# Selective scans in two layers: two groups prepared together, with the bands at other steps

## The chip, the cores and the metric

The kernel runs on one core of a Trainium2 chip. The metric is the device time of one execution in microseconds, and of several executions the median is given. The kernel has four layers; the change touches the selective scans of the first two, which the code calls layer 0 and layer 1.

## The reference, cut to what matters

Both layers contain a two-dimensional selective scan. An image of 56 x 56 tokens is read in four directions: by rows, by columns, and both backwards. For each direction kd, channel d and state n (16 states) the reference does, over the 3136 tokens in turn:

```
dts, Bs, Cs = split(x_proj @ xs)             # per direction
delta = softplus(dt_proj @ dts + bias)
dA    = exp(delta * A[d, n])
h     = dA * h + (delta * x) * B[n]          # the recurrence
y     = sum over n of h * C[n]               # then + D * x
```

Layer 0 does this for two images of 256 channels, one image after the other. Layer 1 has four heads, one after the other; in each, two images of 64 channels lie side by side on the 128 partitions. The layers after these (attention, spectral filters, a mixture of experts) aren't touched.

## The kernel before, in words

The class `Scans` serves both layers. `nch` is the number of blocks of 128 channels: 2 in layer 0, 1 in layer 1. The 3136 tokens of a direction are cut into four quarters of 784 tokens; a direction and a quarter make a *group*, so that one run has 16 groups, in the order of directions 0, 2, 1, 3. Directions 0 and 2 go along rows, 1 and 3 along columns; the latter add their sums to y through a transposed view. A group takes 16 *steps* for each channel block, one step for each state n: 32 steps in layer 0, 16 in layer 1. There are two runs in layer 0 and four in layer 1, 2048 steps in all.

One step, over a tile of 128 x 784, is spread over the engines like this:

- ScalarE makes the decay a = exp(A delta) into one of two PSUM buffers (`decay`, L318).
- TensorE spreads row n of B over the partitions into the PSUM tile b (`spread`, L343). There is one such buffer. VectorE multiplies it by du (L396). For the five states in `POOLED` (2, 5, 8, 11, 14) a DMA brings B's row instead and GpSimd multiplies (L412).
- VectorE runs the recurrence (`scan`, L337).
- ScalarE keeps the last column of h for the next quarter (L329).
- GpSimd multiplies h by C's row, which two DMAs (one in layer 0) have brought, giving p (L409).
- TensorE adds p into the PSUM tile acc by a product with the identity (`add_up`, L357). At a *job boundary*, every 16 steps, ScalarE takes the sum out (L377) and TensorE begins the next one (L371).

The order of instructions on each engine is written out by hand: `emit(s)` issues for step s the decay of step s+1, the scan of s, the spread of s+2, the rows of C for s+3 and of B for s+6, and so on. Each engine takes its own part of that list in order. SP issues the DMAs.

While a group runs, the next one is *prepared*: `pieces_of` gives the pieces, and `preparation` gives each a step, counted from the start of the running group. A piece has place 0 (in the middle of `emit`, with the PSUM tile b as its buffer) or place 2 (at the end of `emit`). The pieces are:

- `rows`: the projection of x to the rows of dt, B and C, taken to SBUF as xd (L161 on TensorE, L173 on ScalarE).
- `keep`: xd goes to DRAM (L177), from which the rows of B and C are read later.
- `fetch`: the rows of B and C come back in another shape, as the tile whole (L184).
- `band` and `rest`: whole is split into three bfloat16 bands that sum to it. `band` casts on ScalarE (L187), `rest` subtracts on GpSimd (L190), and the next band needs that difference.
- `store` and `spread`: the bands go to DRAM (L194) and come back as the tile three (L200), from which TensorE spreads B.
- `steps`: the product for delta (L161), taken out with its bias on ScalarE (L206).
- `soft`: softplus of delta on ScalarE (L209). Softplus and exp are in different tables of ScalarE, so a load stands ahead of it and another ahead of the next exp. In layer 0 the two channel blocks stand together.
- `copy` and `times`: x through the identity into b (L161), and du = delta x on VectorE (L218).

In layer 1 a group has 16 steps, and each group has a preparation of its own with its own softplus.

The pool `rot` gives the tiles delta and du, nch + 1 buffers of each. xd, whole and the bands have one buffer, three has two. The DRAM pool has three buffers for each name.

Of the kernel before, what the change touches and what calls it, by code (L numbers as in the profile page):

```python
# [14 lines left out]
F32 = mybir.dt.float32  # L15
# [15 lines left out]
NS = 16  # L31
# [3 lines left out]
class Chip:  # L35


    def __init__(self, ctx, tc):
        self.tc, self.nc = tc, tc.nc
        nc = tc.nc  # L40
        const = ctx.enter_context(tc.tile_pool(name="const", bufs=1))
        self.ident = const.tile([128, 128], F32, name="ident")
        make_identity(nc, self.ident)
        self.eps = const.tile([128, 1], F32, name="eps")
        nc.gpsimd.memset(self.eps, 1e-5)
        self.one = const.tile([128, 1], F32, name="one")
        nc.gpsimd.memset(self.one, 1.0)
        self.ones = const.tile([1, 128], F32, name="ones")
        nc.gpsimd.memset(self.ones, 1.0)
        self.X = const.tile([TP, NT, B, C], F32, name="X")  # L50
        self._turn = 0
# [54 lines left out]
class Scans:  # L106
# [13 lines left out]
    def __init__(self, k, ctx, nch, row, col, y, w, side=None):  # L120
        tc = k.tc
        self.k, self.nch, self.row, self.col, self.y, self.w = k, nch, row, col, y, w
        self.rot = ctx.enter_context(k.pool("scan0", nch + 1, side=side))
        self.bands = ctx.enter_context(k.pool("scan2", side=side))
        self.threes = ctx.enter_context(k.pool("scan1", 2, side=side))
        self.dram0 = ctx.enter_context(
            tc.tile_pool(name="scan0d", bufs=1, side=side, space=bass.MemoryType.DRAM)
        )
# [8 lines left out]
    def open(self, ctx):  # L137
        k, nch = self.k, self.nch
        self.once = ctx.enter_context(k.pool("scan4", 1))
        self.two = ctx.enter_context(k.pool("scan5", 2))  # L140
        self.hp = ctx.enter_context(k.pool("scanh", 6))
        self.pp = ctx.enter_context(k.pool("scanp", 4))
        self.cp = ctx.enter_context(k.pool("scanc", 4))
        self.bp = ctx.enter_context(k.pool("scanb", 2))
        self.dram = ctx.enter_context(k.tc.tile_pool(name="scand", bufs=3, space=bass.MemoryType.DRAM))
        self.pa = [ctx.enter_context(k.pool(f"pdec{i}", psum=True)) for i in range(2)]
        self.pb = ctx.enter_context(k.pool("prow", psum=True))
        self.pc = ctx.enter_context(k.pool("psum", psum=True))
# [100 lines left out]
        for ci in range(self.nch):  # L249
            f["times"](ci, False)  # L250

    def preparation(self, g):


        f = self.pieces_of(g, lambda name, n: self.once.tile([128, n], F32, name=name), self.dram)
        if self.nch == 1:
            at = [
                (0, 0, "rows", [0, 1]), (3, 0, "steps", 0, [0, 1]), (9, 2, "soft", 0), (12, 0, "copy", 0),
                (12, 2, "times", 0),
            ]  # L260
            s = 1
        else:
            at = [
                (0, 0, "rows", [0]), (3, 0, "rows", [1]), (12, 0, "steps", 0, [0, 1]), (16, 0, "steps", 1, [0, 1]),
                (20, 2, "soft", 0), (20, 2, "soft", 1), (22, 0, "copy", 0), (22, 2, "times", 0), (25, 0, "copy", 1),
                (25, 2, "times", 1),
            ]
            s = 5
        at += [
            (s, 2, "keep"), (s + 2, 2, "fetch"), (s + 4, 2, "band", 0), (s + 4, 2, "rest", 0),  # L270
            (s + 5, 2, "band", 1), (s + 5, 2, "rest", 1), (s + 6, 2, "band", 2), (s + 7, 2, "store"),
            (s + 10, 2, "spread"),
        ]
        return [(t[0], t[1], f[t[2]], t[3:]) for t in sorted(at, key=lambda t: t[0])]

    def on_all(self, pool, g, name, r):

# [11 lines left out]

    def all_steps(self):  # L290
        steps, self.pieces = [], {}
        for i, g in enumerate(self.groups):
            todo = self.preparation(self.groups[i + 1]) if i + 1 < len(self.groups) else []
            for t in todo:
                self.pieces.setdefault((len(steps) + t[0], t[1]), []).append(t)
            for ci in range(self.nch):
                job = dict(g=g, ci=ci)
                steps += [dict(job=job, g=g, ci=ci, n=n, s=len(steps) + n) for n in range(NS)]
        self.state = {}
        self.steps = steps  # L300
        for s in range(-6, len(steps) + 4):
            self.emit(s)
# [1668 lines left out]
```

## Time and profile before

| what | value |
|---|---|
| median of three runs | 9334.89 us (9326.28 to 9335.70) |
| profiled execution | 9324.35 us, span 9322.6 us |
| TensorE busy | 8134.1 us, 87% |
| VectorE busy | 7120.7 us, 76% |
| ScalarE busy | 3895.4 us, 42% |
| GpSimd busy | 6332.5 us, 68% |
| scans of layer 0 | two runs, in about 110 to 1440 and 1500 to 2800 us |
| scans of layer 1 | four runs, between about 2940 and 5910 us |
| softplus (L209) | 128 of 853 ns, 96 table loads of 1283 ns |
| bands (L187) | 270 of 355 ns; idle before: 272.6 us for the subtraction on GpSimd, 223.3 us for the fetch |
| fetch (L184) | 90, median 5.0 us from issue to landing |

The shares of busy time are means over the whole span. The scans take its first two thirds; in these VectorE and GpSimd are busy, later TensorE is. A row of a group gives the number of instructions, the busy time, the mean length of one, and the idle time of the engine just before them with what ended it. "us to landing" runs from the issue of a DMA to its arrival.

### The profile page before, as it was taken

The page shows a single profiled execution, that of the slowest core. Times are in us where ns is not written, and L with a number is a line of the kernel's source. Part 1 is how long each engine was busy: PE and PEld are TensorE (multiplying, and loading weights), DVE is VectorE, ACT ScalarE, POOL GpSimd, SP SyncE. Part 2 cuts the span into 40 slices and gives each one's busy share as a digit, 9 for nine tenths or more (in the row PEclk, how much of TensorE's full clock was granted, in tenths as well). Part 3 has the DMA queues.
Part 4 walks back from the last instruction along what each step waited for, and adds up shares of the span by engine and source line. Part 5 has one row for each costly group of instructions (what it writes and reads, how often), then busy time and mean ns, then how long its engine had stood idle before and what let it go on. Part 6 is the DMA issues. An engine that isn't in the chain of part 4 may idle for free.

```text
span 9322.6 us, 94373 instructions
## 1 busy us (share of the span) xinstructions
PE 8134.1 (87%) x28825; PEld 4783.3 (51%) x28825; DVE 7120.7 (76%) x7587; ACT 3895.4 (42%) x6609; POOL 6332.5 (68%) x4023
## 2 busy tenths in 40 slices
PE   7888888888888888888888888699999999999998
PEld 3444445444444434444443444345588888874555
DVE  8999998999996997998899799711366676765442
ACT  4555545555545555554555555333211111114331
POOL 5999996999994996998799699666411111115551
PEclk9999999999998999999999899699999999999998
DMA  5666664666663884886688488200233333320003
GB/s 156 221 221 215 215 205 132 221 220 215 213 214 93 224 214 127 221 219 168 173 222 214 124 222 215 77 6 4 61 97 104 101 102 95 109 61 7 14 5 127
DMA packets 781383, 1364.60 MB, mean 146 GB/s; under 512 B 133213, under 2 KB 406494, under 8 KB 780842
## 3 DMA queue, kind: packets, MB, share of 16 engines
q1 hardware_dynamic: 780874, 1358.56, 50.8%
q8 instruction: 229, 3.75, 0.2%
q14 instruction: 280, 2.29, 0.1%
HBM read 1318.63 MB, written 39.60 MB: 146 GB/s over the span
## 4 chain that ended last, share of the span: by engine, by line
PE 49%; DVE 21%; issue 12%; ACT 9%; POOL 4%; DMA 4%; SPq 1%; DVEq 0%; POOLq 0%; ACTq 0%
PE cv L1499 12%; DVE h L337 10%; PE acc L357 7%; DVE h L396 7%; PE av L1011 5%; PE sc L1017 5%; PE pj L1613 4%; ACT a L318 3%; PE b L161 3%; DMA c<-rows 2%; PE acc L371 2%; POOL p L409 2%; PE pcv L438 1%; PE b L343 1%; DMA whole<-rows 1%
## 5 line engine op out<-in xcount | busy, mean ns | idle before, releaser
L409 POOL TENSOR_TENSOR p<-h,c 128x784 f32<-128x784 f32 x2048 | 3763.0, 1861 | 232.9 <-PE acc L357 157.4
L357 PE MATMUL acc<-p,ident 128*128 128x392 f32 x8192 | 3133.6, 513 | 88.8 <-POOL p L409 85.1
L337 DVE TENSOR_TENSOR_SCAN h<-a,state,h 128x784 f32<-128x784 f32 x1536 | 2798.0, 1841 | 86.1 <-ACT a L318 64.9
L357 PEld LDWEIGHTS acc<-p,ident 128*128 128x128 f32 x8192 | 1518.0, 197 | 1179.9 <-POOL p L409 200.9
L396 DVE TENSOR_TENSOR h<-du,b 128x784 f32<-128x784 f32 x1408 | 1335.8, 949 | 177.0 <-PE b L343 173.1
L318 ACT ACTIVATE a<-delta,L0A 128x784 f32<-128x784 f32 x1024 | 938.8, 919 | 837.7 <-DVE h L337 835.8
L412 POOL TENSOR_TENSOR h<-du,b 128x784 f32<-128x784 f32 x640 | 1188.9, 1858 | 3.4 <-DMA b<-rows 3.4
L343 PE MATMUL b<-three,sel 96*128 96x512 bf16 (+1 forms) x2816 | 709.3, 333 | 547.7 <-DVE h L396 503.1
L318 ACT ACTIVATE a<-delta,L1A 128x784 f32<-128x784 f32 x1024 | 936.5, 917 | 534.0 <-DVE h L337 531.8
L1030 POOL TENSOR_TENSOR total<-total,e 128x448 f32<-128x448 f32 (+1 forms) x644 | 734.8, 1141 | 328.3 <-ACT e L1019 289.0
L337 DVE TENSOR_TENSOR_SCAN h<-a,h 128x784 f32<-128x784 f32 x512 | 902.0, 1780 | 44.1 <-ACT a L318 27.5
L1512 DVE TENSOR_TENSOR u<-u,cv 128x512 f32<-128x512 f32 x1024 | 623.8, 682 | 326.9 <-PE cv L1499 325.6
L343 PEld LDWEIGHTS <-sel 96*128 96x128 bf16 x2816 | 276.3, 98 | 1159.9 <-issue 919.7
L1543 POOL TENSOR_TENSOR u<-u,S 128x1024 f32<-128x1024 f32 x64 | 150.1, 2367 | 1043.6 <-DVE S L1512 1043.6
L1019 ACT ACTIVATE e<-sc 128x448 f32<-128x448 f32 (+1 forms) x700 | 376.9, 542 | 727.9 <-PE sc L1017 596.0
L1514 ACT COPY u<-cv 128x512 f32<-128x512 f32 x256 | 149.3, 586 | 827.0 <-PE cv L1499 773.4
L1613 PE MATMUL pj<-u,Wm 128*128 128x196 f32 (+8 forms) x1536 | 354.3, 384 | 5.7 <-DVE A L1619 5.7
L1017 PE MATMUL sc<-big 128*128 128x448 f32 (+1 forms) x700 | 324.0, 549 | 12.3 <-ACT e L1019 12.3
L1011 PE MATMUL av<-e,big 128*128 128x448 f32 (+1 forms) x700 | 322.4, 547 | 1.1 <-DVE e L1024 1.0
L187 ACT CAST bands<-whole 128x196 bf16<-128x196 f32 x270 | 95.8, 355 | 531.3 <-POOL whole L190 272.6
L1593 POOL TENSOR_TENSOR both<-mpm 128x512 f32<-128x512 f32 x32 | 40.6, 1268 | 390.3 <-DVE Wm L1649 271.7
L1613 PEld LDWEIGHTS pj<-u,Wm 128*128 128x128 f32 x1536 | 268.4, 192 | 71.4 <-issue 46.0
(438 smaller groups left out, 10998.0 us busy)
## 6 DMA issues: line engine op xcount, KB each, us to landing
c<-rows SPq DMA_DIRECT2D x1024, 392.0 KB, 4.0
c<-rows SPq DMA_DIRECT2D x2048, 196.0 KB, 4.4
b<-rows SPq DMA_DIRECT2D x320, 392.0 KB, 4.5
b<-rows SPq DMA_DIRECT2D x640, 196.0 KB, 4.5
H<-raw SPq DMA_DIRECT2D x32, 1568.0 KB, 7.4
wC<-win SPq DMA_DIRECT2D x64, 576.0 KB, 6.3
w<-in_L_weight_dram SPq DMA_DIRECT2D x52, 512.0 KB, 5.3
wA<-win SPq DMA_DIRECT2D x64, 384.0 KB, 5.3
```

Of the source, the lines that this page charges most:

```text
L318: self.k.nc.scalar.activation(x["a"], g["delta"][ci], AF.Exp, scale=self.w["A"](g["kd"], ci, x["n"]))
L337: self.k.nc.vector.tensor_tensor_scan(h, a, h, start, ALU.mult, ALU.add)
L343: self.k.nc.tensor.matmul(ps[:, c0:c1], lhsT=self.w["selB"](x["n"]), rhs=x["g"]["three"][:, c0:c1], start=True, stop=True)
L357: nc.tensor.matmul(job["acc"][:, i, 0:392], lhsT=self.k.ident, rhs=x["p"][:, 392 * i : 392 * (i + 1)], start=False, stop=n == NS - 1,)
L396: nc.vector.tensor_tensor(one["h"], one["g"]["du"][one["ci"]], one["b"], ALU.mult)
L409: nc.gpsimd.tensor_tensor(now["p"], now["h"], now["c"], ALU.mult)
L412: nc.gpsimd.tensor_tensor(three["h"], three["g"]["du"][three["ci"]], three["b"], ALU.mult)
L1011: nc.tensor.matmul(acc, lhsT=V[b][:n, j, :], rhs=e[:n], start=j == 0, stop=j == NKT - 1)
L1017: nc.tensor.matmul(ps[:n], lhsT=keys[b][:, KT * j : KT * j + n], rhs=q, start=True, stop=True)
L1030: nc.gpsimd.tensor_tensor(total[:n], total[:n], e[:n], ALU.add)
L1499: self.k.nc.tensor.matmul(ps[:, b], lhsT=v[:, C * b : C * (b + 1)], rhs=h, start=i == 0, stop=i == len(terms) - 1)
L1613: nc.tensor.matmul(ps[:, lo - c0 : hi - c0], lhsT=Ws[f][:, eo, r, :], rhs=u[:, b, f, lo - a0 : hi - a0], start=f == 0, stop=f == 1,)
```

## The change

In layer 1 the groups after the first are prepared two at a time, during the 32 steps of the two groups before; the first group, with 16 steps, hosts the preparation of the next two. Both softplus pieces of a pair stand at one step, so that one visit to the softplus table serves two groups. The last group is a set of its own. In both layers the bands come later after their fetch and stand two steps apart (in layer 1's first set, the first of the two keeps them one step apart). The buffers grow to match: three of delta and du in layer 1 too, four in DRAM.

```diff
-        self.rot = ctx.enter_context(k.pool("scan0", nch + 1, side=side))
+        self.rot = ctx.enter_context(k.pool("scan0", 3, side=side))
...
-        self.dram = ctx.enter_context(k.tc.tile_pool(name="scand", bufs=3, space=bass.MemoryType.DRAM))
+        self.dram = ctx.enter_context(k.tc.tile_pool(name="scand", bufs=4, space=bass.MemoryType.DRAM))
...
-    def preparation(self, g):
-        f = self.pieces_of(g, lambda name, n: self.once.tile([128, n], F32, name=name), self.dram)
-        if self.nch == 1:
-            at = [
-                (0, 0, "rows", [0, 1]), (3, 0, "steps", 0, [0, 1]), (9, 2, "soft", 0), (12, 0, "copy", 0),
-                (12, 2, "times", 0),
-            ]
-            s = 1
-        else:
-            at = [
-                (0, 0, "rows", [0]), (3, 0, "rows", [1]), (12, 0, "steps", 0, [0, 1]), (16, 0, "steps", 1, [0, 1]),
-                (20, 2, "soft", 0), (20, 2, "soft", 1), (22, 0, "copy", 0), (22, 2, "times", 0), (25, 0, "copy", 1),
-                (25, 2, "times", 1),
-            ]
-            s = 5
-        at += [
-            (s, 2, "keep"), (s + 2, 2, "fetch"), (s + 4, 2, "band", 0), (s + 4, 2, "rest", 0),
-            (s + 5, 2, "band", 1), (s + 5, 2, "rest", 1), (s + 6, 2, "band", 2), (s + 7, 2, "store"),
-            (s + 10, 2, "spread"),
-        ]
-        return [(t[0], t[1], f[t[2]], t[3:]) for t in sorted(at, key=lambda t: t[0])]
+    def preparation(self, groups, short):
+        def bands(keep, fetch, band, apart, store, spread):
+            yield from ((keep, 2, "keep"), (fetch, 2, "fetch"), (store, 2, "store"), (spread, 2, "spread"))
+            for i in range(3):
+                yield band + apart * i, 2, "band", i
+                if i < 2:
+                    yield band + apart * i, 2, "rest", i
+
+        def du(at, ci):
+            return [(at, 0, "copy", ci), (at, 2, "times", ci)]
+
+        if self.nch == 2:
+            lists = [[
+                (0, 0, "rows", [0]), (3, 0, "rows", [1]), *bands(5, 8, 11, 2, 16, 19), (12, 0, "steps", 0, [0, 1]),
+                (16, 0, "steps", 1, [0, 1]), (20, 2, "soft", 0), (20, 2, "soft", 1), *du(22, 0), *du(25, 1),
+            ]]
+        elif short:
+            lists = [
+                [(0, 0, "rows", [0, 1]), *bands(1, 3, 5, 1, 8, 11), (3, 0, "steps", 0, [0, 1]), (10, 2, "soft", 0), *du(12, 0)],
+                [(6, 0, "rows", [0, 1]), *bands(7, 9, 12, 2, 17, 20), (9, 0, "steps", 0, [0, 1]), (10, 2, "soft", 0), *du(16, 0)],
+            ]
+        else:
+            lists = [
+                [(0, 0, "rows", [0, 1]), *bands(1, 4, 7, 2, 12, 15), (3, 0, "steps", 0, [0, 1]), (20, 2, "soft", 0), *du(22, 0)],
+                [(6, 0, "rows", [0, 1]), *bands(7, 13, 17, 2, 22, 31), (16, 0, "steps", 0, [0, 1]), (20, 2, "soft", 0), *du(25, 0)],
+            ]
+        at = []
+        for g, todo in zip(groups, lists):
+            f = self.pieces_of(g, lambda name, n: self.once.tile([128, n], F32, name=name), self.dram)
+            at += [(t[0], t[1], f[t[2]], t[3:]) for t in todo]
+        return sorted(at, key=lambda t: t[0])
...
-        for i, g in enumerate(self.groups):
-            todo = self.preparation(self.groups[i + 1]) if i + 1 < len(self.groups) else []
-            for t in todo:
+        more = 2 // self.nch
+        sets = [self.groups[:1]] + [self.groups[i : i + more] for i in range(1, len(self.groups), more)]
+        for i, groups in enumerate(sets):
+            for t in self.preparation(sets[i + 1], i == 0) if i + 1 < len(sets) else []:
                 self.pieces.setdefault((len(steps) + t[0], t[1]), []).append(t)
-            for ci in range(self.nch):
-                job = dict(g=g, ci=ci)
-                steps += [dict(job=job, g=g, ci=ci, n=n, s=len(steps) + n) for n in range(NS)]
+            for g in groups:
+                for ci in range(self.nch):
+                    job = dict(g=g, ci=ci)
+                    steps += [dict(job=job, g=g, ci=ci, n=n, s=len(steps) + n) for n in range(NS)]
```

In the text A and B are the first and the second group of a pair, and steps of a pair's preparation are counted from the start of the 32 steps that host it.

## The prediction

> **What bounds the kernel now.** I read the groups first, then the busy time by stretch, then VectorE's waits in the same stretches, then single groups in the timeline.
>
> The two costliest rows that every scan step passes through (columns: line, engine, operation, tiles, count, busy us, mean ns, idle before and its releaser):
>
> ```profile
> L409 POOL TENSOR_TENSOR p<-h,c 128x784 f32<-128x784 f32 x2048 | 3763.0, 1861 | 232.9 <-PE acc L357 157.4
> ...
> L337 DVE TENSOR_TENSOR_SCAN h<-a,state,h 128x784 f32<-128x784 f32 x1536 | 2798.0, 1841 | 86.1 <-ACT a L318 64.9
> ```
>
> GpSimd and VectorE are matched. The timeline gives the real spacings: a VectorE step with product and scan repeats every 2.62 us, a step with a scan alone (5 of 16) every 1.74 us; GpSimd's products follow one another at 1.81 us. I cut the trace at du (L218), which falls once per preparation, so that each stretch holds whole groups (columns: us; PE, weight loads, VectorE, ScalarE, GpSimd busy; clock; DMA share; GB/s).
>
> ```profile
> 1579.00:2131.00 552.00, 456.54 (x1429) 230.07 (x1428) 538.79 (x394) 284.08 (x500) 541.40 (x309) 0.99 0.69 221
> ...
> 3756.00:4039.00 283.00, 234.57 (x716) 119.82 (x715) 270.30 (x197) 155.59 (x266) 273.92 (x162) 0.94 0.86 225
> ```
>
> The first is layer 0, directions 0 and 2: 7 groups of 32 steps, 78.9 us for 32 steps, prepared with one softplus visit. The second is layer 1, same directions: 7 groups of 16 steps, 80.9 us for 32. The transposed directions 1 and 3 (2294 to 2703, 4080 to 4335) take 81.8 and 85.0 per 32. Both engines are busy over 95%, so what can be won is the few per cent of stalls. VectorE's waits in the four stretches, in the order layer 0 direct, layer 0 transposed, layer 1 direct, layer 1 transposed (total us, times, longest):
>
> ```profile
> DVE h L337 <- ACT a L318: 14.2, 22, 1.1
> ```
> ```profile
> DVE h L396 <- PE b L343: 21.8, 10, 3.0
> ```
> ```profile
> DVE h L337 <- ACT a L318: 9.8, 9, 2.5
> DVE h L337 <- ACT state L329: 1.7, 4, 0.7
> ```
> ```profile
> DVE h L396 <- PE b L343: 15.4, 6, 3.5
> DVE h L337 <- ACT state L329: 3.6, 6, 0.7
> DVE h L337 <- ACT a L318: 3.0, 6, 0.9
> ```
>
> Per 32 steps that is 2.0, 4.7, 3.5 and 7.3 us (with the small rows left out here: 1.9 in the second, 0.9 in the third). Taken off 78.9, 81.8, 80.9, 85.0 this leaves 76.9, 77.1, 77.4, 77.7: one base. So VectorE's work plus its stalls is the time, and layer 1 has 1.5 (direct) and 2.6 us (transposed) more stall per 32 steps than layer 0.
>
> **Where the stalls sit.** Bands, layer 1 (columns: start, us, engine, line, ..., idle before):
>
> ```profile
> 3780.77 0.35 ACT L187 CAST bands<-whole 128x196 bf16<-128x196 f32 x1 [4.47 <-DMA whole<-rows]
> ...
> 3781.97 1.85 DVE L337 TENSOR_TENSOR_SCAN h<-a,state,h 128x784 f32<-128x784 f32 x1 [1.50 <-ACT a L318]
> ```
>
> The first band stands two steps behind its fetch, which was issued at 3775.24 and landed 5.5 us later. ScalarE waits at the band, the next exp is queued behind it, the scan starts 1.50 late. Such a stall appears in every direct group (0.5 to 2.5 us), about 1.3 each, 2.6 per pair. The next bands wait 0.76 and 1.03 us for the subtraction on GpSimd.
>
> The job boundary, transposed:
>
> ```profile
> 3420.71 3.13 PE L371 MATMUL acc<-big,ident 128*128 128x392 f32 x4 [1.37 <-ACT big L377]
> ...
> 3425.26 0.91 ACT L206 ACTIVATE delta<-b,L1dtb 128x784 f32<-128x784 f32 x1 [3.05 <-PE b L161]
> ...
> 3426.92 0.97 DVE L396 TENSOR_TENSOR h<-du,b 128x784 f32<-128x784 f32 x1 [1.92 <-PE b L343]
> ```
>
> The take-out of the last sum, the slow first matmuls of the next, the "steps" product right behind them at step 3, its delta on ScalarE, and only then the single PSUM buffer b is free for the spread that VectorE needs. One such stall per layer-1 group, 15.4/6 = 2.6 us.
>
> The double softplus visit exists already, in layer 0:
>
> ```profile
> 1652.00 1.60 ACT L209 ACTIVATE delta<-delta 128x784 f32<-128x784 f32 x2
> ...
> 1655.87 1.85 DVE L337 TENSOR_TENSOR_SCAN h<-a,state,h 128x784 f32<-128x784 f32 x1 [1.00 <-ACT a L318]
> ```
>
> It takes 1650.71 to 1654.92, 4.2 us with its two table loads, and costs the scan 1.0 in direct groups, nothing in transposed ones, where VectorE has just lost 1.47 at the boundary. A single visit in layer 1 takes 3.4 us and costs 0.3 to 0.7.
>
> **What the skill says.** "ScalarE: Activation LUTs", What ACT_TABLE_LOAD costs: a load takes about 1283 ns plus a drain of about 1380. The trace has 1283 and, between the neighbours, no such drain: exp, load, softplus, load, exp stand with gaps of 0.02 us. I use 1.28. "DMA: Bandwidth & Descriptors", Rules for kernel authors: what reads an earlier DMA's write must wait for its completion, and a fixed cost is hidden by issuing early and waiting late. That is the chain keep, fetch, band; here the fetch's median landing is 5.0 us, well over the 2 us that Anatomy of one DMA fits for its fixed cost.
>
> **The change, part by part**
>
> 1. *Half the visits.* Per layer-1 run 15 visits in the scan loop become 8: 28 fewer in all, 56 table loads, 28 x 2 x 1.28 = 72 us of ScalarE. ScalarE is idle 45% of the stage, so only the stall counts: 1.0 for a double visit against 2 x 0.3 to 0.7. I take nothing.
> 2. *First band later.* Three or four steps behind the fetch instead of two. A wait of 4.5 us falls to about 2 (A) or below nothing (B), and 2 us is what ScalarE has to spare (where nothing else stands between, an exp waits 1.6 us for its scan, and the 4.47 above cost the scan 1.50, so some 3 are free). Gain up to 2.6 per direct pair. The bands two steps apart remove the waits of 1 us on GpSimd.
> 3. *Boundaries.* Of two boundaries in 32 steps only A's keeps "steps" at step 3; B's product is at 16, before the boundary at 18, as in layer 0, where that boundary costs 1.47. Transposed: 2.6 x 2 = 5.2 becomes 2.6 + 1.5 = 4.1. The state and exp rows, 6.6/3 = 2.2 per pair, fall to about 0.5. Gain 2.8 per pair.
> 4. *Crowding.* ScalarE has delta at 16, B's bands at 17, 19, 21 and the visit at 20. Bands are 0.35 us each. The band at 21 stands between exp 22 and exp 23; exp 23 ends 1.45 us after exp 22 and its scan is due 1.84 after, so it is covered; without that cover 0.35 per pair. I keep 0.5 in reserve per pair.
> 5. *DMAs and buffers.* Keeps, fetches, stores and spreads are as many as before. On SP, keep to fetch grows from two steps to three or six, so the queue of c and b rows behind stands less; store follows the last band by one step as before. Spread B at 31 serves step 46. Third delta and du buffers and a fourth DRAM buffer are needed because two groups are prepared while two run; they add no instruction. Nothing.
> 6. *The first group* of each run now hosts two preparations in 16 steps: one more du (0.9), two subtractions (1.0), about 1 of stall: +3 us. The pair before the last group hosts one instead of two: -4.
> 7. *Layer 0.* Its bands move from 9, 10, 11 to 11, 13, 15. Band stalls there are 7.2 us over 7 direct groups, 1.0 each; transposed 0.4.
>
> Sum. GpSimd limits the direct gain: 42 products at 1.81 and 4 subtractions at 0.51 are 78.0 per pair, so I put direct pairs at 79.0, 1.9 less. Transposed pairs: 2.6 less. Per layer-1 run: three direct pairs 5.7, a mixed one 2.2, two transposed 5.2, the last 4, first group -3: 14 us, times four 56. Layer 0: 0.6 x 8 + 0.3 x 7 = 7 per run, two runs 14. In all 70 us: the profiled execution, 9324.35 (span 9322.6), goes to 9254. It lies 10.5 below the median of the three runs, 9334.89; taken off the median, 9265. I say 9263.
>
> **Rivals**
>
> - *GpSimd is the bound in direct groups.* It idles 9 us in seven groups, 2.6 per pair, mostly under "PE acc". If those gaps stay, direct pairs gain nothing: mixed 1, transposed 5.2, last 4, first -3 make 7 x 4 = 29, layer 0 about 4: 9302. For it: 97% busy. Against: the gaps come at the end of a group, where it has caught up with the scan, so they follow VectorE.
> - *More of the stall goes.* Direct at GpSimd's 78.0, transposed at 81, layer 0 at 77.3: about 93 + 28 = 120, 9214.
> - *Slower.* ScalarE between steps 16 and 22. If the later bands keep their stalls (the wait moves along with the fetch) and the double visit, with two bands beside it, costs 1.0 + 0.7 against 0.9 for two singles, each of 30 pairs loses 0.8 and each first group 3: +36, 9371. It decides once a visit's stall passes what bands and boundaries save, some 2 us a pair. Layer 0's 1.00 speaks against.
> - *No effect.* The stalls reappear elsewhere, since two matched engines absorb them: 9320 to 9345.
>
> **Numbers.** Likeliest 0.56 (its own range 9235 to 9290), GpSimd 0.19, more 0.12, none 0.07, slower 0.06. A measurement of this kernel can tell about 0.2%, 19 us. Faster: 0.56 + 0.12 + 0.18 = 0.86; within 0.08; slower 0.06. Leaving out a tenth at each end gives 9218 to 9312.
>
> **What would show it.** Right: L209 with 68 table loads for 96; layer-1 waits of bands on the DMA near nothing; du to du of 79 (direct) and 82 (transposed) per pair; one 2.6 us stall of L396 per transposed pair and one near 1.5. Wrong: direct pairs still near 81 with GpSimd idle as now; exp waits over 1.5 us behind the visit at step 20; new waits of p for c rows; a changed layer 0 by more than 30 us.

## The result and the profile after

The changed kernel takes 9252.55 us in the median (9239.89 to 9259.50), the kernel before 9335.30 in the same comparison. The ratio is 0.9909, with a 95% interval of 0.9891 to 0.9926: 0.9% faster. The forecast was 9263 with a range of 9218 to 9312. The profiled execution went from 9324.35 to 9254.57 us, 69.8 less, where the prediction's sum was 70.

The same two rows of the page as before (the lines of the changed kernel stand 16 further down, so L425 is the product p and L353 the scan):

```profile
L425 POOL TENSOR_TENSOR p<-h,c 128x784 f32<-128x784 f32 x2048 | 3758.3, 1860 | 158.9 <-PE acc L373 91.5
...
L353 DVE TENSOR_TENSOR_SCAN h<-a,state,h 128x784 f32<-128x784 f32 x1536 | 2794.4, 1843 | 35.7 <-POOL h L428 16.2
```

The work is the same to a tenth of a per cent. What has changed is the idle time ahead of it: of GpSimd 74 us less, of these scans 50 us less, and their first releaser is no longer ScalarE's exp but GpSimd. Over all scans of the execution, before and then after (who VectorE waited for, us, times):

```profile
  ACT a L318: 92.4, 123
  ACT state L329: 34.5, 58
```
```profile
  ACT a L334: 31.3, 41
  POOL h L428: 22.0, 55
  ACT state L345: 3.6, 7
```

ScalarE's share (a and state together) fell from 126.9 to 34.9 us; a wait for GpSimd, 22 us where it was 0.5, came in. The bands' own waits, before and then after (who the engine waited for, us, times):

```profile
  POOL whole L190: 272.6, 180
  DMA whole<-rows: 223.3, 78
```
```profile
  POOL whole L190: 142.9, 128
  DMA whole<-rows: 22.9, 28
```

The busy time by stretch, cut again at du (L218) so that each stretch holds whole groups: 7 of layer 0's direct groups, two direct pairs and two transposed pairs of layer 1.

```profile
1580.00:2127.00 547.00, 450.77 (x1431) 228.68 (x1430) 538.79 (x394) 285.67 (x500) 540.92 (x309) 0.99 0.68 223
3808.00:3965.00 157.00, 128.79 (x407) 64.17 (x406) 153.16 (x112) 84.12 (x148) 155.58 (x93) 1.00 0.92 229
4125.00:4287.00 162.00, 137.04 (x402) 66.51 (x401) 153.73 (x113) 83.29 (x143) 154.58 (x90) 0.96 0.88 220
```

VectorE's waits in the last two of them, direct and transposed:

```profile
DVE h L353 <- POOL h L428: 2.5, 5, 0.9
DVE h L353 <- ACT a L334: 1.3, 2, 0.8
```
```profile
DVE h L412 <- PE b L359: 7.7, 3, 3.1
DVE h L353 <- ACT a L334: 0.3, 1, 0.3
```

In the direct pairs GpSimd is now busy for 155.6 of 157 us. In the transposed pairs only the job boundaries are left: three waits with 7.7 us in two pairs, 3.9 per pair, where it was 5.1 (15.4 over three). The two behind A's product, still at step 3, are 2.86 and 3.08 us, the third is 1.72, and the fourth boundary shows none.

For the comparisons that follow I use the distance from one du of A to the next, which is the time for 32 steps. The table gives its medians over all runs of the layer in the profiled execution (where layer 1 prepares single groups: over two groups). The times are medians of each kernel's runs; the kernel before ran beside each of them and had medians of 9328.8 to 9335.3, so that differences of a few us between the rows say nothing.

| kernel | time, us | layer 0 direct | layer 0 transposed | layer 1 direct | layer 1 transposed |
|---|---|---|---|---|---|
| before | 9335.3 | 78.9 | 82.0 | 80.7 | 85.0 |
| changed | 9252.6 | 78.2 | 82.1 | 79.0 | 82.0 |
| layer 0's bands back | 9257.5 | 78.9 | 82.0 | 79.2 | 81.8 |
| two visits | 9253.8 | 78.2 | 82.1 | 78.8 | 82.1 |
| B's product at 19 | 9278.2 | 78.2 | 82.1 | 79.6 | 83.5 |
| tight bands | 9300.2 | 78.2 | 82.1 | 80.9 | 84.6 |
| one step apart | 9332.8 | 78.2 | 82.1 | 82.7 | 85.3 |
| early but apart | 9299.7 | 78.2 | 82.1 | 81.1 | 83.6 |
| no subtraction | 9238.2 | 77.9 | 82.0 | 77.8 | 81.8 |
| off the boundary | 9196.5 | 77.9 | 80.2 | 78.9 | 80.6 |
| before, product at 6 | 9298.8 | 78.9 | 82.0 | 80.7 | 81.7 |

### The profile page after: what moved, and what is told of

The parts are those of the page before. It is cut to its first block, busy times and chain, and to the rows that moved or that the text cites. A ratio compares the mean times of both kernels' runs of the same rounds, so it can differ in the third digit from the quotient of the medians.

```text
span 9252.7 us, 94254 instructions
## 1 busy us (share of the span) xinstructions
PE 8116.6 (88%) x28825; PEld 4759.4 (51%) x28825; DVE 7112.8 (77%) x7587; ACT 3840.2 (42%) x6553; POOL 6326.5 (68%) x4023
## 4 chain that ended last, share of the span: by engine, by line
PE 54%; DVE 23%; issue 12%; ACT 5%; POOL 4%; DMA 1%; SPq 0%; DVEq 0%; POOLq 0%; ACTq 0%
PE cv L1515 13%; DVE h L353 11%; PE acc L373 11%; DVE h L412 7%; PE av L1027 5%; PE sc L1033 5%; PE pj L1629 4%; PE b L161 3%; PE acc L387 2%; PE b L359 2%; PE pcv L454 1%; ACT a L334 1%; POOL p L425 1%; POOL h L428 1%; PE cv L1577 1%
## 5 line engine op out<-in xcount | busy, mean ns | idle before, releaser
L425 POOL TENSOR_TENSOR p<-h,c 128x784 f32<-128x784 f32 x2048 | 3758.3, 1860 | 158.9 <-PE acc L373 91.5
L353 DVE TENSOR_TENSOR_SCAN h<-a,state,h 128x784 f32<-128x784 f32 x1536 | 2794.4, 1843 | 35.7 <-POOL h L428 16.2
L373 PEld LDWEIGHTS acc<-p,ident 128*128 128x128 f32 x8192 | 1489.4, 194 | 1298.5 <-POOL p L425 372.6
L353 DVE TENSOR_TENSOR_SCAN h<-a,h 128x784 f32<-128x784 f32 x512 | 901.8, 1780 | 26.2 <-ACT a L334 15.5
L972 DVE TENSOR_REDUCE m<-lo 112x1 f32<-112x448 f32 x392 | 229.3, 618 | 95.1 <-PE lo L968 94.9
```

Of the source, the lines that this page charges most:

```text
L353: self.k.nc.vector.tensor_tensor_scan(h, a, h, start, ALU.mult, ALU.add)
L373: nc.tensor.matmul(job["acc"][:, i, 0:392], lhsT=self.k.ident, rhs=x["p"][:, 392 * i : 392 * (i + 1)], start=False, stop=n == NS - 1,)
L425: nc.gpsimd.tensor_tensor(now["p"], now["h"], now["c"], ALU.mult)
```

## The experiments

My theory: the gain is the bands' (direct groups) and the boundaries' (transposed groups), and the halved softplus visits bring nothing. The rivals: the visits bring it, since 72 us of table loads are removed; or the bands bring all of it.

**Two softplus visits.** This gives the removed visits back, and nothing else.

```diff
-[(0, 0, "rows", [0, 1]), *bands(1, 4, 7, 2, 12, 15), ..., (20, 2, "soft", 0), *du(22, 0)],
+[(0, 0, "rows", [0, 1]), *bands(1, 4, 7, 2, 12, 15), ..., (9, 2, "soft", 0), *du(22, 0)],
```

> The changed kernel with two softplus visits for a pair: A's softplus back at step 9, B's at step 20; 28 visits and 56 table loads more, nothing else. My theory, that a visit's cost is hidden or the same either way: 9253 to 9263, direct pairs 78.6 to 79.1. Rival 'the visits': the 72 us of table loads come back in good part, 9290 or more, pairs 1.3 or more longer.

Measured: 9253.8 us (ratio to before 0.9911, 0.9897 to 0.9926), against 9252.6 with one visit, and pairs of the same length. The rival falls: the 56 table loads and their 72 us of ScalarE don't show in the time. Sharing one visit between two groups, the most visible part of the change, is worth nothing here. A visit isn't free of stalls, but they come out alike: in a direct pair (means over 12) the double visit makes the scan of step 22 wait 0.6 us for its exp, and two single ones make it wait 0.2 there and 0.6 at step 11.

**Tight bands.** Layer 1's bands at the old distances, in the pairs.

```diff
-*bands(1, 4, 7, 2, 12, 15)   # A
+*bands(1, 3, 5, 1, 8, 15)
-*bands(7, 13, 17, 2, 22, 31) # B
+*bands(7, 13, 15, 1, 22, 31)
```

> The changed kernel with layer 1's bands at the old distances: first band two steps behind its fetch, bands one step apart, for A and B; layer 0 and layer 1's first set as changed. My theory: direct pairs go back from 78.6 to 80.5 to 81.2, with scans waiting for exps behind the bands; transposed pairs lose 0 to 0.7; in all 9285 to 9295. Rival 'the visits': at most 9260.

Measured: 9300.2 us, 47.6 more; direct pairs 80.9, as before the change, and transposed ones 84.6, which is 2.6 and much more than the 0 to 0.7 expected. So in the changed kernel the bands pay in both kinds of groups. To see which of the two distances it is, each was taken back alone.

**One step apart.** The first band stays late; only the distance between bands goes back to one step.

```diff
-*bands(1, 4, 7, 2, 12, 15)
+*bands(1, 4, 7, 1, 12, 15)
-*bands(7, 13, 17, 2, 22, 31)
+*bands(7, 13, 17, 1, 22, 31)
```

> The changed kernel with layer 1's first bands where the change puts them (three and four steps behind the fetch) but the next two bands one step apart instead of two; layer 0 and layer 1's first set as changed. If the fetch's landing is what mattered (my theory), little comes back: 9253 to 9263, direct pairs 78.5 to 79.2. If the wait for the subtraction on GpSimd mattered, a good part of the 47 us that the tight bands cost comes back: 9275 or more.

Measured: 9332.8 us (ratio to before 1.0004, 0.9995 to 1.0013). All of the gain is gone; my theory had put it at 9253 to 9263, some 70 us less. The wait for the landing did go, as this row for the bands shows (us, times), but the wait for the subtraction took its place:

```profile
  POOL whole L190: 314.5, 166
  DMA whole<-rows: 24.5, 30
```

One preparation in the timeline (start, us, engine, line, ..., idle before):

```profile
3876.84 0.56 POOL L190 TENSOR_TENSOR whole<-whole,bands 128x196 f32<-128x196 f32 x1
...
3877.44 0.35 ACT L187 CAST bands<-whole 128x196 bf16<-128x196 f32 x1 [3.06 <-POOL whole L190]
...
3880.96 0.57 POOL L190 TENSOR_TENSOR whole<-whole,bands 128x196 f32<-128x196 f32 x1
...
3881.56 0.35 ACT L187 CAST bands<-whole 128x196 bf16<-128x196 f32 x1 [2.95 <-POOL whole L190]
...
3882.84 1.85 DVE L353 TENSOR_TENSOR_SCAN h<-a,state,h 128x784 f32<-128x784 f32 x1 [1.48 <-ACT a L334]
```

The first band has run at 3873.20, with hardly a wait. Its subtraction stands behind GpSimd's products and starts 3.3 us after the band has ended; the next band waits 3.06 for it, the one after 2.95, and the scan starts 1.48 late. In the kernel before these waits were only 1.1 us (means over 24 preparations in direct groups). There the first band had waited 4.4 us for the landing, and the subtraction started 1.4 us after its band, here 3.0 and 3.2. Two steps behind the first band GpSimd's product started 0.7 us after its scan had ended there, and 2.6 to 2.9 here. I read this as GpSimd catching up while the landing holds up the scans.

The wait alone doesn't explain the size of the loss, though. Of the 3.7 us that a direct pair loses (means over 12 pairs), 0.8 lie in its first 16 steps, where A's bands are, and 2.9 in the second 16, with B's. There the last band, held up by the subtraction, runs into the softplus visit of step 20:

```profile
3906.49 0.35 ACT L187 CAST bands<-whole 128x196 bf16<-128x196 f32 x1 [2.84 <-POOL whole L190]
...
3907.78 1.28 ACT L209 ACT_TABLE_LOAD   x1
...
3912.94 1.79 DVE L353 TENSOR_TENSOR_SCAN h<-a,h 128x784 f32<-128x784 f32 x1 [2.52 <-ACT a L334]
```

The scans of steps 21 and 22 wait 1.3 and 2.5 us for their exps in the mean, where the changed kernel has 0 and 0.6. The kernel before has no visit at this distance behind its bands, so the run doesn't say what the subtraction's wait costs away from one; A's half, at 0.8, is the nearest to it.

**Early but apart.** The other half: the first band again two steps behind its fetch, the bands two steps apart.

```diff
-*bands(1, 4, 7, 2, 12, 15)
+*bands(1, 4, 6, 2, 12, 15)
-*bands(7, 13, 17, 2, 22, 31)
+*bands(7, 13, 15, 2, 22, 31)
```

> The changed kernel with layer 1's first band again only two steps behind its fetch (A fetch 4, bands 6, 8, 10; B fetch 13, bands 15, 17, 19), but the bands two steps apart as changed. The runs so far gave +47 us for both distances back at the old values and +80 for the spacing alone, so the wait for the landing and the wait for the subtraction stand in for one another. If the prediction's reading holds in part (the landing alone costs a direct pair 1 to 2.4 us), 9270 to 9300 and direct pairs of 79.5 to 81. If only the spacing matters, 9250 to 9262 and direct pairs of 78.5.

Measured: 9299.7 us, 47 more, direct pairs 81.1; the bands wait 157.6 us for the landing. Here too nearly all of it lies in the second 16 steps of a pair, 1.8 us against 0.1 in the first: A's first band waits only 1.1 us for its landing, B's 4.8, with a late scan behind it:

```profile
3875.43 0.35 ACT L187 CAST bands<-whole 128x196 bf16<-128x196 f32 x1 [4.57 <-DMA whole<-rows]
...
3876.64 1.79 DVE L353 TENSOR_TENSOR_SCAN h<-a,h 128x784 f32<-128x784 f32 x1 [1.55 <-ACT a L334]
```

So either distance taken back alone costs as much as both together (47.6), or more. What isn't separated is the wait from its place: each edit also moves the bands to other steps, and in both runs most of the loss is B's, whose bands stand beside the product at step 16, the boundary and the visit at step 20.

**The bands alone in the kernel before.**

```diff
-            s = 1
+            fetch, band, apart, store, spread, s = 3, 6, 2, 10, 13, 1     # layer 1
...
-            s = 5
+            fetch, band, apart, store, spread, s = 8, 11, 2, 16, 19, 5    # layer 0
...
```

> The kernel before with the later bands alone: in both layers the first band stands three steps behind its fetch and the bands two steps apart; every group of layer 1 keeps its own preparation, its own softplus visit and its product for delta at step 3. My theory (bands pay in the directions along rows, boundaries in the transposed ones, visits nothing): layer 1 takes about 79.0 us per 32 steps in the direct groups (80.9 before, 78.6 with the whole change) and stays at 83.7 to 84.7 in the transposed ones; in all about 9283. Rival 'the visits': layer 1 stays at 80.9 and 84.7, only layer 0 gains, about 9320. Rival 'the bands are everything': 78.6 and 81.9, about 9253.

Measured: 9701.9 us (ratio 1.0393, 1.0377 to 1.0408), 4% slower than before, which none of the theories had. My edit made it so, as TensorE's and VectorE's waits for three show:

```profile
3092.03 0.53 SPq L200 DMA_DIRECT2D three<-bands  x1
...
3097.58 0.84 PE L343 MATMUL b<-three,sel 96*128 96x512 bf16 x2 [8.11 <-DMA three<-bands]
...
3098.45 0.97 DVE L396 TENSOR_TENSOR h<-du,b 128x784 f32<-128x784 f32 x1 [6.56 <-PE b L343]
```

Three is read from step 14 on, and I had issued it at step 13; it lands 5.5 us later, VectorE loses 6.56. Once per preparation, 60 times, this is about 390 us; VectorE's wait for B's row rose by as much, from 173.1 to 566.4 us, and 370 were lost. So the run says nothing on layer 1's bands. It suggests why they were moved together with the pairs: at these distances the chain from keep to three doesn't fit the 16 steps of a single group. Narrower ones weren't tried. In the kernel before three was issued at step 11 and TensorE already waited 0.8 to 1.3 us for it in places. Layer 0, which has 32 steps, took the same edit without harm: 78.2.

**B's product at step 19.**

```diff
-*bands(7, 13, 17, 2, 22, 31), (16, 0, "steps", 0, [0, 1])
+*bands(7, 13, 17, 2, 22, 31), (19, 0, "steps", 0, [0, 1])
```

> The changed kernel with B's product for delta at step 19, right behind the second job boundary, instead of step 16. My theory: the transposed pairs lose what the prediction put on the boundary, 1.1 to 2.6 us (82.9 to 84.5 instead of 81.9), the direct pairs nothing; in all 9265 to 9285. Rivals 'the visits' and 'the bands are everything': nothing changes, 9253.

Measured: 9278.2 us, 25.6 more; transposed pairs 1.5 longer, direct ones 0.6. The boundary is confirmed in the transposed groups. The loss in the direct groups wasn't expected. It stands behind the visit: delta now comes out of TensorE right ahead of step 20, and the scan of step 22 waits 1.6 us for its exp (mean of 12 direct pairs), 0.6 in the changed kernel. The edit doesn't keep this apart from the boundary, so in the transposed pairs too a part of the 1.5 may be the visit's.

**The product at step 6, alone in the kernel before.** This one keeps the early bands and the single visits.

```diff
-(0, 0, "rows", [0, 1]), (3, 0, "steps", 0, [0, 1]), (9, 2, "soft", 0), (12, 0, "copy", 0),
+(0, 0, "rows", [0, 1]), (6, 0, "steps", 0, [0, 1]), (9, 2, "soft", 0), (12, 0, "copy", 0),
```

> The kernel before with one edit: layer 1's product for delta at step 6 instead of 3, away from the job boundary; its own softplus visit at step 9 for every group and the early bands stay. My theory gives the boundary 1.1 us per transposed group, 2.2 per 32 steps (84.7 to 82.5), and nothing in the direct groups: about 9317. Rival 'the bands are everything': no change, 9335. Against both: delta at step 6 and bands at 5 to 7 crowd ScalarE, and it may be slower by up to 20.

Measured: 9298.8 us (ratio 0.9965, 0.9952 to 0.9978), 30 less than before with a single number changed. The direct groups stay at 80.7 for two, the transposed ones go from 85.0 to 81.7. Two boundaries are thus worth 3.3 us in 32 steps, 1.6 each, and "the bands are everything" falls. In the transposed groups this one number brings as much as the whole change does (82.0), although the first bands still wait 4.3 us there for their landing. VectorE's waits over six transposed groups (4080 to 4326) show one of at most 1.4 us at each boundary, where it was 15.4 us in six with up to 3.5:

```profile
DVE h L396 <- PE b L343: 6.6, 6, 1.4
DVE h L337 <- ACT state L329: 3.4, 5, 0.9
DVE h L337 <- ACT a L318: 3.1, 7, 0.7
```

Sixteen such pairs would be 53 us. From the first to the last scan of each run, layer 1's four runs are 47 us shorter in the profile, but the whole execution only 24: the first of them starts 7 us later, and the three pauses between them are 113 us long instead of 104 to 108. Why is open.

**Off the boundary.** The change keeps one product of layer 1 (A's, step 3) and one of layer 0 (rows, step 3) behind a boundary. This moves them too, and with them B's rows and keep and layer 0's chain from keep to three.

```diff
-[(0, 0, "rows", [0, 1]), *bands(1, 4, 7, 2, 12, 15), (3, 0, "steps", 0, [0, 1]), ...],
-[(6, 0, "rows", [0, 1]), *bands(7, 13, 17, 2, 22, 31), ...],
+[(0, 0, "rows", [0, 1]), *bands(1, 4, 7, 2, 12, 15), (6, 0, "steps", 0, [0, 1]), ...],
+[(9, 0, "rows", [0, 1]), *bands(10, 13, 17, 2, 22, 31), ...],
...
-(0, 0, "rows", [0]), (3, 0, "rows", [1]), *bands(5, 8, 11, 2, 16, 19), ...       # layer 0
+(0, 0, "rows", [0]), (6, 0, "rows", [1]), *bands(7, 10, 13, 2, 18, 21), ...
```

> The changed kernel with the last products taken away from the step behind a job boundary: in layer 1 A's product for delta at step 6 instead of 3 (and B's rows and keep at 9 and 10 instead of 6 and 7), in layer 0 the second half of the rows at step 6 instead of 3 (keep, fetch, bands, store and spread two steps later). My theory, that a product right behind the boundary holds the PSUM tile b: a transposed stall of 2.6 to 2.8 falls to the 1.5 of a boundary without one; transposed pairs 80.7 instead of 81.9, layer 0's transposed groups 80.7 instead of 82.0; some 12 and 13 of them with those stalls: 9225 to 9240. Rival: the slow matmuls of the boundary themselves are what is waited for, and nothing changes, 9253. Direct groups unchanged in both.

Measured: 9196.5 us, ratio to before 0.9858 (0.9842 to 0.9875): it beats the kernel before, which ran beside it at 9328.8, by 132 us and the changed one by 56, and lies 28 below the expected 9225. Layer 1's transposed pairs take 80.6 us, as expected; layer 0's transposed groups 80.2, 0.5 better than expected, and its direct ones are 0.3 shorter, where nothing was expected. Between the profiles (68.7 us) layer 0's two runs give 37 and layer 1's four 16; the other 16 lie outside the runs' scans and weren't followed up. VectorE's waits over four transposed groups of layer 0, first the changed kernel (2290 to 2617), then this one (2263 to 2583):

```profile
DVE h L412 <- PE b L359: 19.4, 8, 3.3
```
```profile
DVE h L412 <- PE b L359: 9.6, 7, 2.2
DVE h L412 <- POOL h L428: 0.6, 1, 0.6
DVE h L353 <- ACT a L334: 0.5, 2, 0.3
```

The granted clock in these stretches is 0.94 and 0.98, so TensorE's own work was shorter as well; how much of the 0.5 comes from that isn't separated.

**No subtraction.**

```diff
         def rest(i):
-            nc.gpsimd.tensor_tensor(g["whole"], g["whole"], g["bands"][:, i, :], ALU.subtract)
+            return
```

> The changed kernel without the two subtractions on GpSimd per preparation, so that the second and third band repeat the first (the rows of B are wrong, nothing else is left out). If GpSimd bounds the direct pairs now (78.0 of 78.6 us; four subtractions are 2.0), they fall by 0.8 to 1.5 us to VectorE's base of 77.3 or a little above, layer 0's direct groups (two subtractions, 1.0) from 78.2 to 77.4 to 77.8, the transposed ones by 0 to 0.5: 9220 to 9240. If VectorE bounds them, nothing changes: 9248 to 9258.

Measured: 9238.2 us, 14 less than with the change. Against the kernel before beside each, the two ratios are 0.9901 and 0.9909 with intervals that overlap, so the spacings have to tell. Direct pairs fall by 1.2 to 77.8, layer 0's direct groups by 0.3 to 77.9, the transposed ones hardly. The edit takes two things away: work of GpSimd, and ScalarE's wait for it at the bands (142.9 us in all). The trace speaks for the first: the scans' wait for GpSimd's h falls from 22.0 to 4.4 us, that for ScalarE's a doesn't fall (31.3 and 37.6). So GpSimd does bound the direct pairs of layer 1 now in part: taking 2.0 us of its work off a pair gives 1.2 back, and 77.8 is near the base of 76.9 to 77.7 that the prediction worked out for VectorE.

**Layer 0's bands back.**

```diff
-(3, 0, "rows", [1]), *bands(5, 8, 11, 2, 16, 19), (12, 0, "steps", 0, [0, 1]),
+(3, 0, "rows", [1]), *bands(5, 7, 9, 1, 12, 15), (12, 0, "steps", 0, [0, 1]),
```

> The changed kernel with layer 0's bands at the old steps (fetch 7, bands 9, 10, 11, store 12, spread 15). The two profiles differ by 5.6 us at the start of layer 1, where the prediction had 14: direct groups of layer 0 back from 78.2 to 78.8, transposed ones unchanged at 82.0, in all 9254 to 9264; layer 1 unchanged.

Measured: 9257.5 us, 4.9 more, within the scatter of both kernels. In the trace the direct groups go back to 78.9 and the transposed ones stay.

## Why the prediction was right, point by point

1. *Visits, taken at nothing.* Right. The trace counts 68 loads for L209 instead of 96, and two visits instead of one move the time by 1.2 us, within scatter. At 1.28 us each the loads removed are 72 us; with the drain that the Trainium skill counts ("ScalarE: Activation LUTs", What ACT_TABLE_LOAD costs, 2.66 us a switch) they would be an estimated 149. Neither shows in the time.
2. *First band later, "up to 2.6 per direct pair", and the bands apart as an extra.* The size was right, the reason was half. Direct pairs were put at 79.0 and measured 79.0. But the step read the landing as the cause and the waits of 1 us on GpSimd as an addition. The runs show that the later first band is worth nothing without the distance between the bands, and the reverse (80 and 47 us lost). The second wait looked small because the first one stood ahead of it. That B's bands would also have to clear the visit at step 20 is where most of these losses lie, and it stands in the prediction only under crowding.
3. *Boundaries.* A boundary without the product was put 1.1 us below one with it; the product moved alone gives 1.6 in the kernel before, and its return 1.5 in the changed one. The transposed pair was put at 2.6 to 2.8 shorter and is 3.0 shorter. One stall of about 2.6 and one near 1.5 were forecast for each pair; in two pairs there are 2.9, 3.1, 1.7 and none. The state and exp rows, 2.2 to 0.5 per pair, measured 0.15. But the parts aren't a sum: the tight bands cost a transposed pair 2.6 and the product 1.5, more than 3.0 together, and the product alone in the kernel before gains 3.3 with the bands as they were.
4. *Crowding, 0.5 in reserve.* About right as the change stands: behind the visit the scan of step 22 waits 0.6 us per direct pair, well under the 1.5 that was named as a sign of being wrong. But the place is tight, as the bands one step apart (2.5 there) and the product at 19 (1.6) show.
5. *DMAs and buffers at nothing.* The order of SP held; in the two direct pairs p waited 0.8 us for rows of C. The three buffers of delta and du add no instruction. No run tests it by itself.
6. *First group +3, last pair -4.* Between the starts of scans the first group takes 43.2 us where it took 42.2 (means of four runs), so 1 and not 3; the pair that hosts one preparation takes 79.8 where those two groups took 84.8, so 5. Layer 1 as a whole gave 61 us of the 70: its last scan ends at 5844.4 us instead of 5911.4, and its first starts 5.4 earlier. The prediction had 56.
7. *Layer 0, 14 us.* Too high: 5.4 between the profiles, 4.9 between the medians with its bands moved back, which is within the scatter. The direct groups gave what was said, 0.6 to 0.7 each. The transposed ones gave none of the 0.3, and the turn from direct to transposed groups took 2 us of it back in the first run. Some 4 more went in the pause between the two runs (131.1 and 134.8 us), which varies between 131 and 137 where this code is the same.
8. *GpSimd as the limit of the direct pairs.* Right: 99% busy, and the run without subtractions shows it. As a rival it had said that the gaps stay and nothing is won there; most of the gaps went (9.1 us in seven groups before, 1.4 in two pairs now), as the prediction argued, because they followed VectorE.

That the sum came out at 70 against 69.8 is in part luck: layer 0 gave 8 to 9 us less than said, layer 1 some 5 more, and 3 came from behind the scans, where nothing was forecast. One count in the rival "slower" is off: four runs have 28 double visits, not 30, which makes it 34 us and not 36.

## What to carry to other kernels

A wait is named after what ended last. Before it is priced, ask what else would be late in its place: here a wait for a landing stood ahead of a wait for a subtraction on a full engine, and taking away either alone, with the visit as near as it was, lost over half of the gain or all of it. The 56 table loads fewer on an engine with slack changed nothing that could be measured; a piece of side work that shares the only buffer with the main chain costs by its place, and one changed step number, away from a job boundary, gave 30 us alone.

## What the runs showed of the hardware that I had not expected

The granted clock of TensorE in layer 0's transposed groups rose from 0.94 to 0.98 when the products left the boundary, with nearly the same number of matmuls in the two stretches (815 and 821). In the kernel that issued three at step 13 the mean clock over the execution was 0.926 against 0.951 before, although TensorE waited longer for three. The runs don't say what sets it.
